# Emission order and per-tag buffer counts in a four-layer graph network kernel

## The chip, the cores and the metric

One Trainium2 chip, one core. The metric is the device time of one execution in microseconds (us). Lower is better. The kernel was already tuned. All runs told of here were in the same (fast) state, every kernel's output was correct, and each kernel has four timed runs (the kernel before, which was timed again with every call, seven in each later call).

A word on names. TensorE (PE in the profile) does the products and the transposes, VectorE (DVE) and ScalarE (ACT) do elementwise work, GpSimd (POOL) does a few small things. A *group* is four of the 128 graphs; there are 32 groups. An *accumulator* is one PSUM bank that a product writes and another engine reads. A *tag* is a name under which a pool keeps a ring of buffers: the n-th request for a tag with k buffers takes the place of request n - k, and must wait until that one is no longer used. An fp32 product shows as two matmul records in the trace, so a record count of 8 there means four products; a transpose shows as one record (the eight of a group's features as x8). The *granted clock* is the share of TensorE's full speed that the chip allowed it, as the trace records it.

## The reference, cut to what matters

Each of 128 graphs has 128 nodes with 256 features and an integer adjacency matrix. Four layers follow one another, each with a residual and a layernorm:

```python
x = _layernorm(x + _L0(x, adj, a0..a3))       # scores (x*a_k) x^T per edge type, softmax, times x
x = _layernorm(x + _L1(x, adj, W_msg, W_upd, bias))  # relu(x W_upd + mean of messages + bias)
x = _layernorm(x + _L2(x, adj, weight, w_ih, w_hh, ...))  # three GRU steps; each: aggregate A^T h, gates
x = _layernorm(x + _L3(x, adj, W, a))         # graph attention: softmax, times x W, elu
```

Within one graph everything depends on what went before. Different graphs are independent.

## The kernel before

All accumulators come from one PSUM tag with eight banks. All SBUF tiles of a group come from a pool with two buffers per tag unless a tile says otherwise.

```python
    work = ctx.enter_context(tc.tile_pool(name="work", bufs=2))
    psum = ctx.enter_context(tc.tile_pool(name="psum", bufs=8, space=bass.MemoryType.PSUM))

    def bank():
        return psum.tile([P, 512], F32, tag="ps", name="ps")
    ...
    def features_first(xn):                       # eight transposes, two banks
        xT = work.tile([P, KC, T], F32, tag="xT", name="xT")
        for c in range(KC):
            ps = bank()
            for b in range(G):
                nc.tensor.transpose(ps[:, b * N : (b + 1) * N], xn[:, b, c * P : (c + 1) * P], ident)
            ...
```

A group is a generator. It yields wherever TensorE would have to wait for another engine, and a small driver alternates between two groups that stand at different points:

```python
    def group(g):
        ...
        xT = features_first(xg)
        xs = work.tile([P, G, KC, 4, N], F32, tag="xs", name="xs", bufs=1)
        yield
        ...                                # scaled features, four edge types
        yield
        ...                                # scores, softmax, layernorm; layer 1; layernorm
        for i in range(NL):                # three recurrent steps
            ...                            # aggregation: 8 products of 128x128
            for c in range(KC):
                p_hn = gate(2 * KC + c, True, False)
                yield
                p_r = gate(c, True, True)
                ...
                yield
                p_in = gate(2 * KC + c, False, True)
                ...
        ...                                # layer 3

    STAGGER = 16
    running, g, step = [], 0, 0
    while running or g < NG:
        if g < NG and step >= g * STAGGER and len(running) < 2:
            running.append(group(g))
            g += 1
        for r in list(running):
            try:
                next(r)
            except StopIteration:
                running.remove(r)
        step += 1
```

## Time and profile before

| | before |
|---|---|
| time, median of 4 runs | 3757.63 us (3757.21 to 3757.7) |
| TensorE busy / idle in the span of 3756.9 us | 3353.8 / 403.1 us |
| granted TensorE clock, mean | 0.949 |
| one group, in the pairing (prediction's working) | about 116 us |

What TensorE waited for, from the view of waits of the kernel before. The columns are: what waited, what it waited for, us in all, how many times, and the longest.

```profile
PE ps L189 <- DVE xb L177: 163.7, 32, 8.6
PE ps L211 <- ACT prob L203: 77.3, 48, 4.0
PE ps L189 <- DVE xa L177: 67.8, 42, 4.5
PE ps L385 <- DVE hT L373: 29.3, 48, 2.1
```

There are 96 layernorms followed by transposes, 64 softmaxes and 96 ends of a recurrent step in the whole run. So the second column from the right shows how often the other group failed to cover: of the 96 step ends (L385) only 48 show a wait, of 0.6 us on average.

### The profile page before, as it was taken

What the parts mean: (1) busy time and instruction counts of PE and PEld (TensorE: products, weight loads), DVE (VectorE), ACT (ScalarE), POOL (GpSimd) and SP (SyncE); (2) the same over time, 40 slices, a digit from 0 to 9 for tenths busy, and PEclk for the clock granted to TensorE, in tenths of its full rate; (3) what the DMA queues carried; (4) which work ended last, traced back from release to release, by engine and by line L of the source; (5) the groups of instructions that cost most, each with busy time, mean ns of one, the idle gap of its engine ahead of it and who ended that gap; (6) DMA issues with size and microseconds to landing.
All of it is one profiled execution on the core that took longest, in us unless ns stands there. A gap on an engine that the chain in (4) does not pass through costs nothing.

```text
span 3756.9 us, 30963 instructions
## 1 busy us (share of the span) xinstructions
PE 3353.8 (89%) x10708; PEld 1804.6 (48%) x10708; DVE 2012.7 (54%) x5232; ACT 972.9 (26%) x2004; POOL 504.9 (13%) x487
## 2 busy tenths in 40 slices
PE   6998989889898898989989799898998989989896
PEld 4444444545454444545445444444444544445453
DVE  3456464564645546465464645546455464564644
ACT  2222222222222222232222222223222222222222
POOL 0111111111111111111111111111111111111111
PEclk8999999999999999999999899999999999999998
DMA  2000000000000000000000000000000000000000
GB/s 69 9 8 21 0 20 9 12 17 1 20 9 12 18 6 15 8 15 14 6 20 3 18 11 6 20 3 20 9 12 17 1 20 9 12 12 0 12 1 12
DMA packets 56957, 47.48 MB, mean 13 GB/s; under 512 B 4320, under 2 KB 56672, under 8 KB 56800
## 3 DMA queue, kind: packets, MB, share of 16 engines
q1 hardware_dynamic: 56800, 45.50, 3.9%
q8 instruction: 85, 1.39, 0.1%
q14 instruction: 72, 0.59, 0.0%
HBM read 28.72 MB, written 16.78 MB: 12 GB/s over the span
## 4 chain that ended last, share of the span: by engine, by line
PE 77%; DVE 14%; ACT 3%; issue 2%; POOL 2%; POOLq 0%; DVEq 0%; ACTq 0%
PE ps L342 48%; PE ps L290 6%; PE ps L250 6%; PE ps L328 5%; PE ps L189 4%; PE ps L406 3%; DVE st L170 2%; PE ps L385 2%; POOL rstd L174 2%; DVE hT L373 1%; DVE res L307 1%; PE ps L211 1%; DVE neg L441 1%; PE ps L437 1%; ACT t_z L368 1%
## 5 line engine op out<-in xcount | busy, mean ns | idle before, releaser
L342 PE MATMUL ps<-agT,c_gi 128*128 128x512 f32 x2304 | 1072.8, 595 | 0.0
L342 PE MATMUL ps<-hT,w_hhT 128*128 128x512 f32 x1536 | 753.2, 608 | 0.0
L342 PEld LDWEIGHTS ps<-agT,c_gi 128*128 128x128 f32 x2304 | 439.6, 191 | 552.4 <-issue 537.1
L372 DVE SCALAR_TENSOR_TENSOR t_d<-t_z,t_d 128x512 f32<-128x512 f32 x192 | 132.9, 692 | 501.7 <-ACT t_z L368 465.2
L342 PEld LDWEIGHTS ps<-hT,w_hhT 128*128 128x128 f32 x1536 | 280.7, 197 | 218.4 <-issue 214.8
L342 PE MATMUL ps<-xT,w_hhT 128*128 128x512 f32 x768 | 359.0, 593 | 0.0
L354 DVE TENSOR_SCALAR t_r<-t_r 128x512 f32<-128x512 f32 x192 | 81.6, 425 | 500.6 <-ACT t_r L353 500.6
L371 POOL TENSOR_TENSOR t_d<-hT,t_n 128x512 f32<-128x512 f32 x128 | 162.1, 1266 | 1031.8 <-ACT t_n L362 1031.8
L353 ACT ACTIVATE t_r<-ps,brz 128x512 f32<-128x512 f32 x192 | 131.6, 685 | 648.4 <-PE ps L342 648.4
L362 ACT ACTIVATE t_n<-t_r,bih 128x512 f32<-128x512 f32 x192 | 138.4, 721 | 455.5 <-DVE t_r L360 455.4
L290 PE MATMUL ps<-w_um,xT 128*128 128x512 f32 x512 | 231.2, 595 | 0.5 <-ACT xT L191 0.5
L250 PE MATMUL ps<-xs,xT 128*128 128x512 f32 x512 | 230.1, 592 | 1.7 <-ACT xs L245 1.7
L368 ACT ACTIVATE t_z<-ps,brz 128x512 f32<-128x512 f32 x192 | 131.3, 684 | 379.2 <-PE ps L342 379.2
L342 PEld LDWEIGHTS ps<-xT,w_hhT 128*128 128x128 f32 x768 | 142.3, 192 | 153.1 <-issue 145.8
L174 POOL TENSOR_TENSOR rstd<-rstd,neg_half 128x4 f32<-128x4 f32 x128 | 130.6, 1020 | 608.2 <-DVE rstd L173 603.2
L189 PE MATMUL ps<-ident,xb 128*128 128x128 f32 x256 | 53.4, 357 | 163.7 <-DVE xb L177 163.7
L258 DVE COPY_PREDICATED alpha<-mk,ps 128x128 f32<-128x128 uint8 x512 | 153.2, 300 | 81.4 <-PE ps L250 68.1
L191 ACT COPY xT<-ps 128x512 f32<-128x512 f32 x128 | 74.6, 583 | 420.6 <-PE ps L189 420.5
L360 DVE SCALAR_TENSOR_TENSOR t_r<-t_r,ps 128x512 f32<-128x512 f32 x192 | 131.5, 685 | 82.9 <-PE ps L342 79.2
L203 ACT ACTIVATE prob<-alpha,nmax 128x128 f32<-128x128 f32 x256 | 99.7, 391 | 264.6 <-DVE nmax L199 264.6
L371 POOL TENSOR_TENSOR t_d<-xT,t_n 128x512 f32<-128x512 f32 x64 | 81.0, 1266 | 620.3 <-ACT t_n L362 620.3
L406 PE MATMUL ps<-w3x,xT 128*128 128x257 f32 x512 | 153.7, 448 | 7.4 <-ACT xT L191 7.4
(95 smaller groups left out, 4045.0 us busy)
## 6 DMA issues: line engine op xcount, KB each, us to landing
x_in<-in_x_dram SPq DMA_DIRECT2D x32, 512.0 KB, 3.8
out_dram<-xb SPq DMA_DIRECT2D x32, 512.0 KB, 2.9
adj_in<-in_adj_dram SPq DMA_DIRECT2D x32, 256.0 KB, 2.8
nat<-in_L_gnn_w_hh_dram SPq DMA_DIRECT2D x1, 768.0 KB, 5.1
nat<-in_L_gnn_w_ih_dram SPq DMA_DIRECT2D x1, 768.0 KB, 6.8
wnat<-in_L_gnn_weight_dram SPq DMA_DIRECT2D x1, 768.0 KB, 7.7
w_um<-in_L_gnn_W_upd_dram SPq DMA_DIRECT2D x1, 256.0 KB, 3.4
w_um<-in_L_gnn_W_msg_dram SPq DMA_DIRECT2D x1, 256.0 KB, 3.6
```

The source lines that it names most:

```text
L174: nc.gpsimd.tensor_tensor(rstd, rstd, neg_half, OP.pow)
L189: nc.tensor.transpose(ps[:, b * N : (b + 1) * N], xn[:, b, c * P : (c + 1) * P], ident)
L250: nc.tensor.matmul(ps, xT[:, c, b * N : (b + 1) * N], xs[:, b, c].rearrange("p k n -> p (k n)"), start=(c == 0), stop=(c == KC - 1),)
L258: nc.vector.copy_predicated(alpha0[:, b, :], mk[:, k, b, :], ps[:, k * N : (k + 1) * N])
L290: nc.tensor.matmul(ps, xT[:, c, b * N : (b + 1) * N], w_um[:, c, :], start=(c == 0), stop=(c == KC - 1))
L328: nc.tensor.matmul(ps[:, b * N : (b + 1) * N], hn[:, b, c * P : (c + 1) * P], a_ne[:, b, :], start=True, stop=True,)
L342: nc.tensor.matmul(ps, w[:, q * P : (q + 1) * P], v, start=(n == 0), stop=(n == len(terms) - 1))
L362: nc.scalar.activation(t_n, t_r, AF.Tanh, bias=bih[:, 2 * KC + c : 2 * KC + c + 1], scale=1.0)
L368: nc.scalar.activation(t_z, p_z, AF.Tanh, bias=brz[:, KC + c : KC + c + 1], scale=0.5)
L371: nc.gpsimd.tensor_sub(t_d, hT[:, c, :], t_n)
L372: nc.vector.scalar_tensor_tensor(t_d, t_z, 1.0, t_d, op0=OP.add, op1=OP.mult)
L406: nc.tensor.matmul(ps[:, : D + 1], xT[:, c, b * N : (b + 1) * N], w3x[:, c, :], start=(c == 0), stop=(c == KC - 1),)
```

## The change

Its intent, in the words that came with it: groups emitted whole, oldest first, with buffers counted by tag so that three groups are in flight instead of two in lockstep. It has three parts: the yields and the driver go; every SBUF tag gets a buffer count of its own; and the scaled features of layer 0 are made in two halves that share one buffer. The core of the diff:

```diff
-    work = ctx.enter_context(tc.tile_pool(name="work", bufs=2))
+    pool = ctx.enter_context(tc.tile_pool(name="work", bufs=2))
...
+    BUFS = dict(
+        x_in=3, adj_in=2, a_f=2, mk=2, a_ne=3, m_gt=4, alpha=2, prob=2, probT=2,
+        xs=1, xT=3, hT=3, agT=3, hn=3, hu=1, x1=2, x2=3, x3=2, y=1, res=2,
+        t_r=3, t_n=3, t_z=2, t_d=2, mv=4, st=6, rstd=4, nmax=4, rsum=4, rinv=4, fac=6,
+    )
... (layer 0)
         xT = features_first(xg)
-        xs = work.tile([P, G, KC, 4, N], F32, tag="xs", name="xs", bufs=1)
-        yield
-        for c in range(KC):
+        for h in range(G // 2):
+            xs = work.tile([P, 2, KC, 4, N], F32, tag="xs", name="xs")
+            ...                        # scale two graphs, then their four score products
... (everywhere)
-        yield
...
-    STAGGER = 16
-    running, g, step = [], 0, 0
-    while running or g < NG:
-        ...
+    for g in range(NG):
+        group(g)
```

The weights' staging tiles also move from a pool of their own into the work pool. The PSUM tag is not touched.

## The prediction

> **What bounds the kernel now.** I read the page's first part and the chain that ended last, then the groups of instructions with the idle time before them, then TensorE's timeline at both ends of the run, then the granted clock by stretch.

> ```profile
> PE 3353.8 (89%) x10708; PEld 1804.6 (48%) x10708; DVE 2012.7 (54%) x5232; ACT 972.9 (26%) x2004; POOL 504.9 (13%) x487
> ...
> PE 77%; DVE 14%; ACT 3%; issue 2%; POOL 2%; POOLq 0%; DVEq 0%; ACTq 0%
> ```

> TensorE is busy for 89% of the span and carries 77% of the chain; the next engine is at 54%. So TensorE's own work is the floor, and about 3757 - 3354 = 403 us of its idle time is what a better interleaving could win. Some 23 us of the work is preparation, so a group of four graphs costs (3354 - 23) / 32 = 104 us of TensorE, and takes (3757 - 37) / 32 = 116 us in the present pairing. Nothing on the page shows what a group costs when no other group fills its waits. But two stretches do: the first group runs alone until the second enters at 91 us, and the last runs alone from 3693 us on. TensorE's timeline of the first (columns: start, length, instruction, and the idle time before it with what ended it):

> ```profile
> 37.14 1.04 PE L189 MATMUL ps<-ident,x_in 128*128 128x128 f32 x8
> 39.84 7.11 PE L250 MATMUL ps<-xs,xT 128*128 128x512 f32 x16 [1.67 <-ACT xs L245]
> 50.32 1.48 PE L211 MATMUL ps<-ident,prob 128*128 128x128 f32 x4 [3.37 <-ACT prob L203]
> 52.48 3.78 PE L271 MATMUL ps<-x_in,probT 128*128 128x256 f32 x8 [0.68 <-ACT probT L213]
> 60.81 1.94 PE L189 MATMUL ps<-ident,xa 128*128 128x128 f32 x8 [4.55 <-DVE xa L177]
> 63.20 8.25 PE L290 MATMUL ps<-w_um,xT 128*128 128x512 f32 x16 [0.46 <-ACT xT L191]
> 71.29 1.90 PE L300 MATMUL ps<-hu,a_f 128*128 128x257 f32 x8
> 80.50 2.10 PE L189 MATMUL ps<-ident,xb 128*128 128x128 f32 x8 [7.31 <-DVE xb L177]
> 82.39 3.62 PE L328 MATMUL ps<-a_ne,xb 128*128 128x128 f32 x16
> 85.80 3.68 PE L342 MATMUL ps<-xT,w_hhT 128*128 128x512 f32 x8
> ```

> Layers 0 and 1 of a lone group make TensorE wait for a softmax (3.37), a layernorm (4.55) and a mean with its layernorm (7.31). The last group, alone in its third recurrent step and layer 3:

> ```profile
> 3692.12 0.88 PE L385 MATMUL ps<-ident,hT 128*128 128x128 f32 x6 [0.68 <-DVE hT L373]
> 3693.53 2.05 PE L328 MATMUL ps<-a_ne,hn 128*128 128x128 f32 x16 [0.53 <-ACT hn L392]
> 3695.41 3.60 PE L342 MATMUL ps<-hT,w_hhT 128*128 128x512 f32 x8
> ...
> 3718.54 0.87 PE L385 MATMUL ps<-ident,hT 128*128 128x128 f32 x6 [2.14 <-DVE hT L373]
> 3723.93 1.97 PE L189 MATMUL ps<-ident,xa 128*128 128x128 f32 x8 [4.51 <-DVE xa L177]
> 3726.36 4.53 PE L406 MATMUL ps<-w3x,xT 128*128 128x257 f32 x16 [0.46 <-ACT xT L191]
> ...
> 3736.63 1.63 PE L211 MATMUL ps<-ident,prob 128*128 128x128 f32 x4 [4.03 <-ACT prob L203]
> 3738.94 3.78 PE L437 MATMUL ps<-wh,probT 128*128 128x256 f32 x8 [0.68 <-ACT probT L213]
> ```

> And the granted clock by stretch (third figure from the end; first row the lone first group, second the paired middle, third the lone last group):

> ```profile
> 37.00:86.00 49.00, 30.80 (x95) 18.70 (x94) 24.81 (x84) 9.06 (x23) 3.38 (x5) 0.76 0.07 17
> 1000.00:1200.00 200.00, 186.31 (x594) 98.79 (x595) 104.28 (x262) 51.07 (x100) 26.97 (x25) 0.97 0.03 10
> 3718.00:3745.00 27.00, 14.50 (x46) 9.71 (x46) 10.93 (x29) 6.35 (x19) 1.15 (x2) 0.69 0.00 1
> ```

> A lone group pays twice: it waits, and the clock falls from 0.97 to 0.76 or 0.69. The same eight transposes take 1.04 us at 37 us, and 1.94 to 2.10 after the long waits.

> [...] TensorE's records of before stand in the order of the built list wherever I compared them, and a waiting transpose (2.98 us at 3683.85) holds up gate products of the other group behind it. So if the list holds one group after another, no product of the next can fill a wait. [...] in half-microsecond stretches the clock is 1.00 or 0.50 but for the slices of a change; it drops at 51.7, returns at 65.0, drops at 75.3, returns at 85.5: about 13.4, 10.3 and 10.2 us apart, near whole multiples of 3.4.

> **The change part by part.** It removes every point where one group hands over to the other, calls the groups one after another, gives each tag its own number of SBUF buffers, and computes the scaled features of layer 0 in two halves through one buffer. The sum of products does not change: 6398 TensorE instructions in both built lists. The order does. The intent is that the scheduler overlaps three groups because their SBUF buffers allow it. But all accumulators are still one PSUM tag of 8 banks. In the built lists of both kernels the 2167 accumulators are first written in exactly the order in which the program asks for them, none out of order. Before, the program asked alternately for two groups. Now it asks for all of a group's banks before the next group's first, and the list of TensorE follows: the last product of group g (L431) comes before the first transpose of group g+1, 31 times of 31. So three groups are in flight only for loads and masks; on TensorE it is one. From group 5 to group 28 the lists of TensorE, VectorE, ScalarE and GpSimd repeat without a difference, so one period times 31 gives the time.

> A period, from the end of one group's last product to the next one's:
> (a) Layer 0 up to its last score product. Alone, at full clock, 39.84 + 7.11 - 37.14 = 9.8 us. Now the lists put the tail of the previous group (ELU, layernorm, output) among it, and VectorE's list puts the second half's scaling (128x256, estimated at 0.3 us from 0.48 for 128x512) behind that layernorm. The lone tail at the end of before starts writing its normalised output 3751.64 - 3742.72 = 8.9 us after the last product. Add about 1.9 because the ELU alternates with the next group's copies and scalings, 0.6 for predicated copies between, 1.4 for the four writes, 1.3 for four more predicated copies, 0.9 for scaling: the second half starts at about 15.0, after a wait of some 7 us, so at half clock. Four products of 0.86 us at full speed then take about 6.0. Estimate 21.0.
> (b) To the first gate product, as in the lone first group: 85.80 - 46.95 = 38.9.
> (c) Three recurrent steps of 24 gate products at 0.858: 3716.18 - 3695.41 = 20.8 each, 62.3.
> (d) Two inner step boundaries: 3718.54 - 3716.18 = 2.4 of wait, then 3695.41 - 3692.12 = 3.3 of transposes, copy and aggregation; 5.7 each, 11.3. [...]
> (e) Last step's end to the last product of layer 3: 3742.72 - 3716.18 = 26.5.
> Sum 161.5 us, against 116 now.

> The first group starts some 5 us later, as the second weight load must now wait for its one staging buffer: about 42. It has layer 0 alone with the halving's own wait (9.8 + 1.4) and b to e (140.5), so it ends at 194. Then 31 x 161.5 = 5006, and the lone tail of 3756.9 - 3742.7 = 14.2. Sum 5214; I say 5200. TensorE's busy share should be about 73%, its clock about 0.84.

> **The rivals.** One: the groups do overlap, as the change intends, and the 403 us of idle time mostly go: 3757 - 350 = about 3400. For it, VectorE's 54% leaves room; against it, the built order, with not one of 31 handovers mixed. Two: the order is serial, but the tail of a group hides fully behind the next one's layer 0 and the clock recovers quickly: (a) becomes about 11 and (d) has no surcharge, 150 a group, about 4850. Against it, the second half's scaling stands behind the previous layernorm in VectorE's list. Three: the waits of 2.4 us at step boundaries drop the clock nearly each time[...], about 5350. For it, the drop at 51.7 came in a window with only about 2.1 us idle; against it, the clock stood at 1.00 through the wait at 3716.4.

> **Range and chances.** All terms but (a) and the surcharge in (d) are read from the same instructions in the same order, at the clock that lone running gives. I leave 5 us a group upward (5214 + 150) and 7 downward (5214 - 217): 5000 to 5380. Faster would need the built order not to be the order run; 0.01. Within 2%: 0.01. Slower: 0.98.

> **What would show it.** In the profile after: TensorE's timeline repeats every 160 us or so with no product of another group within a group; waits of about 3.4, 4.6, 7.3, 2.1, 4.5 and 4.0 us before the softmax and layernorm transposes, once per group each; a wait of about 7 us amid the score products of layer 0; clock near 0.84; VectorE's busy time about unchanged at 2000. The prediction is wrong at its root if score products of one group stand among gate products of another, wrong in (a) if the wait amid the scores is far from 7 us, and wrong in (d) if the waits at step boundaries differ from 2.1 or the aggregation after them takes far over 2.05.

One term is cut: a surcharge of 1.5 us in (d), for waits at step boundaries that lower the clock; it was the author's guess. The sum includes it: 21.0 + 38.9 + 62.3 + 12.8 (11.3 and 1.5) + 26.5 = 161.5 us. What the trace of before shows of order and clock:

- Order: a transpose waited 2.98 us until 3683.85, and the other group's gate products behind it started at 3684.12.
- Clock: the clock record holds 50 stretches at 1.00 and 50 at 0.50, nothing else, and its changes lie on one grid with a step of 3.4133 us (to within 0.001 us). A window, in the prediction, is one such step. The window before the fall that the prediction puts at 51.7 (51.84 in the record) held 2.10 us of idle time.

The allowances in (a) are estimates. The mean durations in the trace of before to hold them against are 0.30 us for a predicated copy (L258), 0.41 for a write of a normalised output (L177) and 0.48 for a scaling of 128x512 (L243).

## The result, and the profile after

| | before | after |
|---|---|---|
| time, median of 4 runs each | 3757.63 us | 5178.01 us (5177.85 to 5180.56) |
| span of the profiled run | 3756.9 us | 5176.3 us |
| TensorE busy | 3353.8 us | 3837.8 us |
| TensorE idle (span less busy) | 403.1 us | 1338.5 us |
| granted clock, mean | 0.949 | 0.842 |

The ratio is 1.378 (95% interval 1.3761 to 1.38). Here and below a ratio is the mean time of one kernel's runs over the mean of the kernel before's runs of the same rounds, so it isn't quite the ratio of the medians. Later the kernel before had medians of 3756.64, 3758.0 and 3758.76 us. All outputs are right.

The page of the kernel after: the line of busy times, and the line of the chain that ended last.

```profile
PE 3837.8 (74%) x10708; PEld 2092.7 (40%) x10708; DVE 2024.9 (39%) x5359; ACT 1007.8 (19%) x2133; POOL 506.2 (10%) x487
...
PE 68%; DVE 19%; ACT 7%; POOL 4%; issue 2%; POOLq 0%; DVEq 0%; ACTq 0%
```

The number of TensorE records is the same, 10708, and VectorE's busy time has moved by 12 us. No work was added or taken away, yet TensorE is 484 us longer busy (3837.8 - 3353.8) and idle for 935 us more (1338.5 - 403.1). Together these are the 1419 us that the span grew. The second is waiting. The first is mostly the same products run at a lower clock, as experiment 5 will show (347 to 435 us of it).

The view of waits of the kernel after, to be laid beside that of before:

```profile
PE ps L205 <- DVE x L193: 509.1, 96, 7.3
PE ps L227 <- ACT prob L219: 237.0, 64, 4.4
PE ps L386 <- DVE hT L375: 204.1, 96, 2.4
PE ps L266 <- DVE xs L259: 198.8, 33, 6.3
PE ps L266 <- ACT xs L261: 55.5, 31, 1.8
```

The counts are now complete: every one of 96 layernorms, 64 softmaxes and 96 step ends makes TensorE wait. And there is a new row, the score products (L266) waiting for the scaled features: 6.3 us, once in every group.

One whole period in TensorE's timeline (start, length, instruction, and in brackets the idle time before it and what ended it). Most gate products and some other rows are left out.

```profile
1054.81 3.86 PE L347 MATMUL ps<-xT,w_hhT 128*128 128x512 f32 x8
...
1078.14 0.88 PE L386 MATMUL ps<-ident,hT 128*128 128x128 f32 x6 [2.08 <-DVE hT L375]
1079.36 3.60 PE L333 MATMUL ps<-a_ne,hn 128*128 128x128 f32 x16 [0.35 <-ACT hn L393]
1082.80 3.60 PE L347 MATMUL ps<-hT,w_hhT 128*128 128x512 f32 x8
...
1105.92 1.00 PE L386 MATMUL ps<-ident,hT 128*128 128x128 f32 x6 [2.14 <-DVE hT L375]
1107.14 3.38 PE L333 MATMUL ps<-a_ne,hn 128*128 128x128 f32 x16 [0.22 <-ACT hn L393]
1110.36 3.60 PE L347 MATMUL ps<-hT,w_hhT 128*128 128x512 f32 x8
...
1138.98 1.97 PE L205 MATMUL ps<-ident,x 128*128 128x128 f32 x8 [4.25 <-DVE x L193]
...
1152.20 1.63 PE L227 MATMUL ps<-ident,prob 128*128 128x128 f32 x4 [4.03 <-ACT prob L219]
1154.50 3.57 PE L431 MATMUL ps<-wh,probT 128*128 128x256 f32 x8 [0.68 <-ACT probT L229]
1157.91 1.04 PE L205 MATMUL ps<-ident,x_in 128*128 128x128 f32 x8
1160.74 4.07 PE L266 MATMUL ps<-xs,xT 128*128 128x512 f32 x8 [1.79 <-ACT xs L261]
1171.14 5.49 PE L266 MATMUL ps<-xs,xT 128*128 128x512 f32 x8 [6.33 <-DVE xs L259]
1179.99 1.48 PE L227 MATMUL ps<-ident,prob 128*128 128x128 f32 x4 [3.37 <-ACT prob L219]
...
1189.98 1.97 PE L205 MATMUL ps<-ident,x 128*128 128x128 f32 x8 [4.43 <-DVE x L193]
...
1209.93 2.10 PE L205 MATMUL ps<-ident,x 128*128 128x128 f32 x8 [7.25 <-DVE x L193]
...
1215.23 3.86 PE L347 MATMUL ps<-xT,w_hhT 128*128 128x512 f32 x8
```

Two things are to be seen. First, the row at 1157.91: the next group's first transposes come straight after the last product (L431) of the group before, and no product of one group stands among another's (the 332 TensorE matmul records from one group's first transposes to the next one's come in the same order 32 times of 32). Three groups are not in flight on TensorE; one is. Second, the aggregation (L333) takes 3.60 and 3.38 us after waits of 2.08 and 2.14 us. The same work took 2.05 us in the last group of before, at full clock.

In stretches of half a microsecond around these two aggregations, the third figure from the end is the granted clock:

```profile
1079.00:1079.50 0.50, 0.15 (x2) 0.14 (x1) 0.45 (x1) 0.31 (x1) 0.00 (x0) 0.72 0.00 0
1079.50:1080.00 0.50, 0.50 (x3) 0.50 (x4) 0.24 (x1) 0.00 (x0) 0.00 (x0) 0.50 0.00 0
...
1082.50:1083.00 0.50, 0.50 (x5) 0.49 (x4) 0.00 (x1) 0.00 (x0) 0.00 (x0) 0.86 0.00 0
...
1106.50:1107.00 0.50, 0.43 (x3) 0.06 (x1) 0.04 (x1) 0.49 (x1) 0.00 (x0) 0.53 0.00 0
...
1109.50:1110.00 0.50, 0.50 (x4) 0.50 (x4) 0.00 (x0) 0.32 (x1) 0.00 (x0) 0.56 0.00 0
```

A mean of 0.72 over 0.5 us is 0.22 us at full clock and 0.28 at half, so the clock fell at about 1079.22; worked out in the same way from the other rows it came back at 1082.64, fell again at 1106.53 and came back at 1109.94. Each stay at half clock lasts 3.41 or 3.42 us, and the falls are 27.31 us apart, eight times 3.41. So each of these two short waits is followed by one stay of 3.41 us at half clock, and the stays lie on one grid. The trace's clock record bears this out for the whole run: 252 stretches at 1.00 and 252 at 0.50, no other share, and all their changes on one grid with a step of 3.4133 us (to within 0.001 us); the kernel before has the same step. I call one step of this grid a window. The aggregation falls into it.

### The profile page after: what moved, and what is told of

Read it like the earlier page. It is cut to its first block, busy times and chain, and to the rows that moved or that the text cites. A ratio compares the mean times of both kernels' runs of the same rounds, so it can differ in the third digit from the quotient of the medians.

```text
span 5176.3 us, 31348 instructions
## 1 busy us (share of the span) xinstructions
PE 3837.8 (74%) x10708; PEld 2092.7 (40%) x10708; DVE 2024.9 (39%) x5359; ACT 1007.8 (19%) x2133; POOL 506.2 (10%) x487
## 4 chain that ended last, share of the span: by engine, by line
PE 68%; DVE 19%; ACT 7%; POOL 4%; issue 2%; POOLq 0%; DVEq 0%; ACTq 0%
PE ps L347 38%; PE ps L333 6%; PE ps L301 5%; PE ps L205 4%; PE ps L266 3%; DVE st L186 3%; PE ps L404 3%; POOL rstd L190 3%; PE ps L431 2%; PE ps L285 2%; DVE alpha L274 2%; POOL res L440 1%; DVE t_d L374 1%; ACT prob L219 1%; DVE hT L375 1%
## 5 line engine op out<-in xcount | busy, mean ns | idle before, releaser
L347 PE MATMUL ps<-hT,w_hhT 128*128 128x512 f32 x1536 | 701.1, 592 | 0.0
L205 PE MATMUL ps<-ident,x 128*128 128x128 f32 x768 | 193.1, 431 | 509.1 <-DVE x L193 509.1
L266 PE MATMUL ps<-xs,xT 128*128 128x512 f32 x512 | 299.7, 728 | 258.0 <-DVE xs L259 198.8
L205 PEld LDWEIGHTS ps<-ident,x 128*128 128x128 f32 x768 | 145.4, 213 | 557.6 <-DVE x L193 299.4
L373 POOL TENSOR_TENSOR t_d<-hT,t_n 128x512 f32<-128x512 f32 x128 | 162.2, 1267 | 1603.5 <-ACT t_n L365 1603.5
L386 PE MATMUL ps<-ident,hT 128*128 128x128 f32 x768 | 137.0, 308 | 204.1 <-DVE hT L375 204.1
L266 PEld LDWEIGHTS ps<-xs,xT 128*128 128x128 f32 x512 | 111.1, 234 | 427.6 <-issue 331.9
L301 PE MATMUL ps<-w_um,xT 128*128 128x512 f32 x512 | 272.2, 693 | 14.8 <-ACT xT L207 14.8
L227 PE MATMUL ps<-ident,prob 128*128 128x128 f32 x256 | 94.4, 402 | 242.4 <-ACT prob L219 237.0
L333 PE MATMUL ps<-a_ne,hn 128*128 128x128 f32 x1024 | 219.8, 402 | 17.9 <-ACT hn L393 17.9
L333 PEld LDWEIGHTS ps<-a_ne,hn 128*128 128x128 f32 x1024 | 207.6, 311 | 37.3 <-ACT hn L393 37.3
```

What stands on the lines that cost most here:

```text
L266: nc.tensor.matmul(ps, xT[:, c, b * N : (b + 1) * N], xs[:, j, c].rearrange("p k n -> p (k n)"), start=(c == 0), stop=(c == KC - 1),)
L301: nc.tensor.matmul(ps, xT[:, c, b * N : (b + 1) * N], w_um[:, c, :], start=(c == 0), stop=(c == KC - 1))
L333: nc.tensor.matmul(ps[:, b * N : (b + 1) * N], hn[:, b, c * P : (c + 1) * P], a_ne[:, b, :], start=True, stop=True,)
L347: nc.tensor.matmul(ps, w[:, q * P : (q + 1) * P], v, start=(n == 0), stop=(n == len(terms) - 1))
L373: nc.gpsimd.tensor_sub(t_d, hT[:, c, :], t_n)
```

## The experiments

The theory: TensorE runs its list in order (the waiting transpose at 3683.85 in the kernel before, and the 31 handovers of 31 in the kernel after, agree); with one PSUM tag, the order of the list is the order in which the program asks for banks; whole emission therefore makes TensorE do the groups one after another, each with all its waits, and the waits lower the clock as well (0.842 against 0.949). The rivals: the buffer counts or the halved scaling cost the time; the clock plays no part; it is some other resource than the banks that keeps the groups apart. Built instruction lists back the premise: in the kernels before and after, the 2167 accumulators are first written exactly in the order of the requests, none out of order.

### 1. Whole emission alone: old buffers, no halving

```diff
 # from the kernel before
-    STAGGER = 16
-    running, g, step = [], 0, 0
-    while running or g < NG:
-        ...
+    for g in range(NG):
+        for _ in group(g):
+            pass
```

> The kernel before with one change: each group's program is emitted to its end before the next one's begins; old buffers (two of each), layer 0's scaling in one piece. Theory (the order in which accumulators of the one PSUM tag are asked for sets TensorE's order, whatever the SBUF buffers are): serial, 5085 us, between 5000 and 5180; it lacks the wait amid layer 0's scores but has a longer one at the softmax behind. Rival (the new buffer counts or the halved scaling cost the time): within 3% of 3757.

Measured: 5064.37 us (5063.34 to 5064.59), ratio 1.3481 (1.3459 to 1.3504), clock 0.828. The order alone brings 1307 or 1308 of the 1420 us (5178.01 - 3757.63). On top of it the buffers and the halving add the other 114. The view of waits of this kernel shows where:

```profile
PE ps L250 <- ACT xs L245: 110.4, 32, 3.5
```

The score products wait 3.5 us once a group, where the kernel after waits 1.8 and 6.3 us, 254 us in all: there the second half of the scaling (L259) stands in VectorE's list behind the previous group's output (`y`, L193), as VectorE's timeline of the kernel after shows:

```profile
1168.09 1.38 DVE L193 TENSOR_SCALAR y<-res,mv,rstd 128x256 f32<-128x256 f32 x4 [1.00 <-POOL rstd L190]
1169.39 0.89 DVE L274 COPY_PREDICATED alpha<-mk,ps 128x128 f32<-128x128 uint8 x4
1170.18 0.35 DVE L259 TENSOR_SCALAR xs<-xT,acol 128x256 f32<-128x256 f32 x1
```

Of this difference of 144 us a part is given back, since TensorE is busy for 3881.6 us here and for 44 us less in the kernel after.

### 2. The new buffers and the halving alone: old order

```diff
 # from the kernel after: the yields and the old driver put back
+        yield
 ...
-    for g in range(NG):
-        group(g)
+    STAGGER = 16
+    while running or g < NG:          # two running, as before
+        ...
```

> The changed kernel with the old emission put back: two groups handing over to each other at the same points; buffers by tag, halved scaling and the new weight staging stay. Theory: 3757 within 2% (3690 to 3830), as nothing but the emission order matters. Rival (buffers and halving cost the time): above 4500.

Measured: 3758.03 us (3754.74 to 3762.24), ratio 1.0005 (0.999 to 1.002), clock 0.949. TensorE's busy time is that of before to within a microsecond, 3353.0 against 3353.8 us.

With two groups in alternation, the counts by tag are worth nothing, good or bad. Experiments 1 and 2 together leave the order as the cause.

### 3. Two PSUM tags by parity of the group

Is it the one ring of banks that fixes the order? Here even and odd groups ask for banks under different tags, four each. Everything is still emitted whole.

```diff
 # from the kernel after
+    lane = [0]
     def bank():
-        return psum.tile([P, 512], F32, tag="ps", name="ps")
+        return psum.tile([P, 512], F32, tag=f"ps{lane[0]}", name="ps", bufs=4)
...
     for g in range(NG):
+        lane[0] = g % 2
         group(g)
```

> The changed kernel with two PSUM tags of four banks, one for even and one for odd groups; SBUF tags still shared. Built list: 93 of 2167 accumulators first written out of emission order, about three a group, all at the handover (scores of layer 0 of the next group ahead of the softmax of layer 3). Theory (both kinds of tag hold the order; here only PSUM is loosened): waits at the handover partly filled, 4900 us, between 4780 and 5050. Rival (the PSUM tag alone is to blame): below 4000.

Measured: 4858.75 us, ratio 1.2935 (1.2915 to 1.2954), clock 0.843. In the built list there are now 93 places where an accumulator is first written after one that was asked for later. The timeline at a handover shows what they are:

```profile
1083.97 1.88 PE L413 MATMUL ps<-xT,w2b 128*128 128x512 f32 x4
1085.69 3.60 PE L268 MATMUL ps<-xs,xT 128*128 128x512 f32 x8
1090.32 1.49 PE L229 MATMUL ps<-ident,prob 128*128 128x128 f32 x4 [1.03 <-ACT prob L221]
...
1093.58 2.84 PE L433 MATMUL ps<-wh,probT 128*128 128x256 f32 x8
...
1106.13 1.63 PE L229 MATMUL ps<-ident,prob 128*128 128x128 f32 x4 [6.27 <-ACT prob L221]
```

The next group's scores (L268) fill the wait for the old group's last softmax (L229): 1.03 us of it is left, against 4.03. But this is given back at the younger group's own softmax, which now waits 6.27 us instead of 3.37, so that the softmax waits stay at 234.6 us in all, against 237.0. What is gained lies elsewhere: the waits amid the scores, 254 us in all in the kernel after, sink to 2.6, and TensorE is busy for 49 us less (3788.5). The younger group gets no farther than the scores of layer 0, since the SBUF tags are still shared by all groups, and the layernorm waits stay at 511.7 us, the step ends at 204.4.

### 4. SBUF tags by parity as well

```diff
 # from experiment 3
     BUFS = dict(
-        x_in=3, adj_in=2, ... xT=3, hT=3, agT=3, ...
+        x_in=1, adj_in=1, ... xT=1, hT=2, agT=1, ...     # mostly one buffer per lane
...
-            return pool.tile(shape, dtype, tag=tag, name=name, bufs=BUFS[tag])
+            return pool.tile(shape, dtype, tag=f"{tag}{lane[0]}", name=name, bufs=BUFS[tag])
```

> The changed kernel with PSUM and SBUF tags both by parity of the group, one buffer of most tags in each set. Groups are still emitted whole. Built list: score, update and aggregation products of a younger group stand among those of the older. Theory: real overlap of two groups, oldest first; TensorE's work of 3354 us plus 100 to 300 of waits: 3550, between 3430 and 3700. Rival (emission of whole groups is bad in itself, alternation is needed): 3757 or more.

Measured: 3996.42 us (3993.68 to 3997.22), ratio 1.0638 (1.0622 to 1.0654), clock 0.917. This missed what I expected, and fell where the rival had put it (3757 or more). The overlap is real: there are 218 such places in the built list, and 1182 of the 1420 us come back with nothing but tags by parity and smaller buffer counts. (The same SBUF lanes over one PSUM tag, which I built but did not run, leave 0 out of order. Both kinds of tag are needed.) But it is slower than the kernel before. Its timeline shows why it falls short:

```profile
1046.68 2.05 PE L270 MATMUL ps<-xs,xT 128*128 128x512 f32 x2 [11.43 <-DVE xs L263]
...
1052.89 3.60 PE L351 MATMUL ps<-xT,w_hhT 128*128 128x512 f32 x8
...
1073.71 2.74 PE L270 MATMUL ps<-xs,xT 128*128 128x512 f32 x6
```

The older group's recurrent steps, which are dense and need no help, run from 1052.89 on with 48 gate records to a step and nothing of the younger group between them; the younger one gets only a few score products where a step ends (1073.71). Then both groups stand in their waiting layers at once, and TensorE waits 11.43 us. The view of waits puts 320.7 us on that one place. "Oldest first" spends the overlap where it isn't needed; that this, and not the single buffers, is the cause is tested in experiment 9.

### 5. Waits filled with unread products

If the lower clock has a share of its own, then keeping TensorE busy in the waits, with products that nobody reads, must make the kernel faster although it adds work.

```diff
 # from the kernel after
+    def keep_warm(n):
+        ps = bank()
+        for _ in range(n):
+            nc.tensor.matmul(ps, w_um[:, 0, :P], w_um[:, 0, :], start=True, stop=True)
 ...   # keep_warm(3) ahead of softmax transposes, 4, 7 and 4 after x1, x2 and x3,
 ...   # 2 and 6 ahead of the halves of the scores, 2 ahead of each step's transposes
```

> The changed kernel with products that nobody reads put in TensorE's list ahead of its waits (2 to 7 of 0.86 us, each lot somewhat shorter than the wait), so that the clock has no reason to fall. Group order and waits stay. Theory: the 1419 us lost are 935 us of waits and 484 us of half clock (busy time 3838 against 3354); with the clock at 1.00 nearly throughout the time is 3354 + 1338 = 4690, between 4620 and 4800. Rival (the clock is only a companion, the waits in the chain set the time): 5178 within 1%.

Measured: 4863.87 us, ratio 1.2946 (1.2924 to 1.2967), clock 0.971. It is 314 us faster than the kernel after, with 1120 more products (two records each). I had expected more. The page, and the row of the unread products in the groups of instructions:

```profile
PE 4429.1 (91%) x12948; PEld 2230.3 (46%) x12948; DVE 2023.5 (42%) x5359; ACT 1005.8 (21%) x2133; POOL 505.7 (10%) x487
```

```profile
L73 PE MATMUL ps<-w_um 128*128 128x512 f32 x2240 | 1026.6, 594 | 0.0
```

Without the unread products, TensorE is busy for 4429.1 - 1026.6 = 3402.5 us, which is 435 less than the 3837.8 of the kernel after and only 49 more than the 3353.8 of before. This is the upper reading: the ends of products are modelled, and for 89 us the unread ones overlap their neighbours. Counted alone, the records of the other products cover 3491.3 us, which is 347 less than in the kernel after. So of the 484 us by which the products had grown longer, 347 to 435 go away when the clock is held up (0.971 against 0.842). With the upper reading, the span gains less because the filling isn't exact: the idle time falls from 1338.5 to 431.9 us, that is by 907, and the filling takes 1027, 120 too much. 435 - 120 = 315 us is the difference of the profiled spans (5176.3 - 4861.0). The expectation was in effect the whole 484 (5178 - 484 = 4694); the overrun of 120 and the 49 that stayed are what it lacked (with the lower reading, an overrun of 31 and 137 that stayed).

### 6. A second buffer for the scaled features

```diff
 # from the kernel after
-        xs=1, xT=3, hT=3, agT=3, ...
+        xs=2, xT=3, hT=2, agT=2, ...
```

> The changed kernel with two buffers for the scaled features of layer 0 (those for hT and agT cut to two). Built list: the second half's scaling now stands ahead of the previous group's layernorm, but the predicated copies of the scores still stand behind it. Theory: the wait of 6.3 us amid the scores goes, and most of it comes back at the softmax, because VectorE reaches the last copies only about 16.5 us after the previous group's last product: 3.5 us a group saved, 5070, between 5000 and 5130. Rival (the one buffer is the cause and its wait is gained whole with its clock, 8 us a group or more): below 4930.

Measured: 4965.72 us, ratio 1.3217 (1.3197 to 1.3237). The wait of 6.3 us amid the scores is gone, and part of it reappears as a longer wait for the softmax behind it:

```profile
1110.43 1.04 PE L205 MATMUL ps<-ident,x_in 128*128 128x128 f32 x8
1113.26 7.50 PE L266 MATMUL ps<-xs,xT 128*128 128x512 f32 x16 [1.79 <-ACT xs L261]
1127.43 1.63 PE L227 MATMUL ps<-ident,prob 128*128 128x128 f32 x4 [6.67 <-ACT prob L219]
```

From the first transposes to the softmax's it is 1127.43 - 1110.43 = 17.0 us here and 1179.99 - 1157.91 = 22.1 in the kernel after: 5.1 saved, where I had expected 3.5. The period fell by more still, 6.83 us, from 160.42 to 153.59; the trace shows the aggregation after the first step's end at 2.05 us instead of 3.60 in 31 of 32 groups, so part of the rest is clock. The time missed both what I expected (5000 to 5130) and the rival (below 4930). That this is twice 3.41 led to experiments 11 and 12.

### 7. Two groups in alternation, half a pass apart

```diff
 # from experiment 2
-    STAGGER = 16
+    STAGGER = 26
```

> Alternating emission of two groups as in the run that put the old order back, but each group starts 26 handovers after the one before it (half of a group's 51), where it was 16 and then 35 by turns. Theory: before's 403 us of idle time come from every second neighbour pair being in its waiting layers together; evenly offset, layers 0, 1 and 3 of one always lie beside the recurrent steps of the other: 3500, between 3420 and 3600. Rival (the offset does not matter): 3757 within 2%.

Measured: 3696.54 us, ratio 0.984 (0.9825 to 0.9854), clock 0.965. A gain of 61 us, clear of its interval, and a quarter of the expected one: idle time is still 344 us (3697.0 - 3353.1). The groups hand over at a count of yields, not of microseconds, so an offset of half the yields isn't half the time; that may be why, but no run shows it, and it stays open.

### 8. Three groups in alternation, new buffers

```diff
 # from experiment 2
-    STAGGER = 16
+    STAGGER = 17
...
-        if g < NG and step >= g * STAGGER and len(running) < 2:
+        if g < NG and step >= g * STAGGER and len(running) < 3:
```

> Alternating emission of three groups, 17 handovers apart, with the new buffer counts: what the change meant to have, three groups in flight. Theory: enough buffers for three; TensorE's idle time falls below that of two evenly offset groups: 3440, between 3390 and 3560. Rival (the counts are too small for three, waits for buffers take the place): 3650 or more.

Measured: 3556.43 us (3555.01 to 3556.98), ratio 0.9465 (0.9451 to 0.9479), clock 0.972: 5.4% faster than before, and the fastest kernel. It lies at the slow end of what I expected (3390 to 3560). Its page:

```profile
PE 3292.1 (93%) x10708; PEld 1786.6 (50%) x10708; DVE 2045.5 (58%) x5359; ACT 995.8 (28%) x2133; POOL 533.1 (15%) x487
```

A few rows of its timeline show gate products (L362) of two groups, one in its first step (its state is xT) and one in a later step (hT), with a third group's first transposes (x_in) ahead of them, and no wait:

```profile
1042.37 1.04 PE L205 MATMUL ps<-ident,x_in 128*128 128x128 f32 x8
1043.24 1.88 PE L362 MATMUL ps<-hT,w_hhT 128*128 128x512 f32 x4
1044.96 1.88 PE L362 MATMUL ps<-agT,c_gi 128*128 128x512 f32 x4
1046.68 1.88 PE L362 MATMUL ps<-xT,w_hhT 128*128 128x512 f32 x4
```

So what the change wanted, three groups in flight, is worth having. It has to be asked for in the order of emission.

### 9. The lanes of experiment 4 with alternating emission

```diff
 # from experiment 4: the yields put back, and
-    for g in range(NG):
-        lane[0] = g % 2
-        group(g)
+    STAGGER = 26
+    ...                               # the driver with two running; before each step
+            lane[0] = r[0]            # of a group, its parity
```

> PSUM and SBUF tags by parity of the group with one buffer of most, exactly as in the run with both kinds of lane, but the emission alternates between two groups 26 handovers apart instead of whole groups. Theory (in the run with lanes the groups were emitted whole, so every older product outranked the younger group's, which crept through layer 0 during the older's recurrent steps and then met it in its waiting layers): with alternation the younger gets its turns, 3690 or a little better, between 3600 and 3750. Rival (single buffers in each lane cost the time): 3950 to 4050 again.

Measured: 3604.88 us, ratio 0.9595 (0.9579 to 0.9611), clock 0.970. With the same tags and the same single buffers as experiment 4, alternating brings 392 us (3996.42 - 3604.88). So it was whole emission, oldest first, that held experiment 4 back, and not its small number of buffers. Tags by parity help under alternation too: experiment 7 alternates with the same offset but shared tags, has more buffers, and is 92 us slower (3696.54).

### 10. Three groups in alternation, old buffers

```diff
 # from the kernel before
-    STAGGER = 16
+    STAGGER = 17
...
-        if g < NG and step >= g * STAGGER and len(running) < 2:
+        if g < NG and step >= g * STAGGER and len(running) < 3:
```

> The kernel before with three groups in flight, 17 handovers apart, in place of two; its two buffers of each tag and its undivided scaling stay. Theory (three groups alternating need the counts of the change): tags with two buffers make the third group's instructions wait in TensorE's list, 3650 to 4000. Rival (only the emission matters, the counts do not): 3556 within 1%.

Measured: 3631.75 us, ratio 0.9666 (0.9652 to 0.9681), clock 0.967. It fell between what I expected and what the rival said. A third group helps even with two buffers a tag, by 3.3%; the counts by tag and the halving then bring a further 75 us (3631.75 - 3556.43; the intervals of the two ratios are far apart), the only place where they paid. With experiments 1, 2 and 8 the picture is a small table (medians in us):

| emission | old buffers | counts by tag, halved scaling |
|---|---|---|
| two in alternation | 3757.6 (before) | 3758.0 (exp. 2) |
| whole, oldest first | 5064.4 (exp. 1) | 5178.0 (after) |
| three in alternation | 3631.8 (exp. 10) | 3556.4 (exp. 8) |

### 11 and 12. One and two more products in every group

The mean period of groups 8 to 24, from the start of one group's first transposes to the next one's, came out near whole multiples of 3.4133 us, the step of the clock record in the kernels before and after, in kernels that differ in much else. These are the kernels whose means came out so:

| kernel | mean period, us | over 3.4133 |
|---|---|---|
| after | 160.421 | 47.00 |
| experiment 1 | 157.002 | 46.00 |
| experiment 3 | 150.186 | 44.00 |
| experiment 4 | 122.88 | 36.00 |
| experiment 6 | 153.588 | 45.00 |
| experiment 7 | 112.638 | 33.00 |

The others did not, or not cleanly: the quotients are 33.75 (before), 33.66 (experiment 2), 31.69 (8), 32.34 (9) and 32.54 (10), and in experiment 5 the mean gives 44.01 but single periods range from 149 to 151 us. So a lock is something that a kernel can have, not something that every kernel has.

If the period is locked to the windows, a little more work in each group costs either nothing or a whole window. So I put one and then two unread products of 0.86 us ahead of the first gate products, where TensorE doesn't wait:

```diff
 # from the kernel after
+            if i == 0:
+                unread = bank()
+                for _ in range(1):          # 2 in the second of the two kernels
+                    nc.tensor.matmul(unread, w_um[:, 0, :P], w_um[:, 0, :], start=True, stop=True)
```

> The changed kernel with one unread product of 0.86 us a group in TensorE's list ahead of the first gate products, where nothing waits. The period of the changed kernel is 160.43 us from group to group, 47.0 of the 3.413 us in which the clock changes, and other runs show 46.0, 45.0, 44.0, 36.0 and 33.0. Theory (each group's length settles on a whole number of clock windows): the period stays at 160.43 (5178 within 8) or becomes 163.84 (5284 within 10). Rival (a chance, work adds up): 5178 + 32 x 0.86 = 5205 within 5.

> The same with two unread products, 1.72 us a group. Theory: a period of 160.43 or 163.84 us, so 5178 within 8 or 5284 within 10. Rival: 5178 + 32 x 1.72 = 5233 within 5.

Measured: 5183.09 us (5181.39 to 5183.75), ratio 1.3793 (1.3773 to 1.3814), and 5192.13 us (5188.57 to 5194.1), ratio 1.3817 (1.3796 to 1.3838). Thirty-two times 0.86 and 1.72 us would be 28 and 55 us; the kernels became 5 and 14 us slower. The mean periods are 160.427 and 160.421, unchanged. The second kernel missed the locked expectation by 6 us, but it is far from the rival's. By the fifth group, before the lock settles, it has fallen 6.1 us behind the kernel after; from there to the thirtieth each group starts 6.08 to 6.14 us later than there, although every one of them has more work; and the last two groups add 6.7 us. Where the time is absorbed, the second kernel's timeline shows:

```profile
1060.90 2.15 PE L355 MATMUL ps<-w_um 128*128 128x512 f32 x4
1062.88 3.60 PE L347 MATMUL ps<-xT,w_hhT 128*128 128x512 f32 x8
...
1085.94 0.88 PE L390 MATMUL ps<-ident,hT 128*128 128x128 f32 x6 [2.08 <-DVE hT L379]
1087.16 2.05 PE L333 MATMUL ps<-a_ne,hn 128*128 128x128 f32 x16 [0.35 <-ACT hn L397]
```

The wait before the aggregation is 2.08 us as before, but the aggregation now takes 2.05 us and not 3.60: it came at another place on the grid and kept the full clock (the granted clock is 1.00 from 1087 to 1089 us). The same holds in 29 of 32 groups. So most of the added 1.7 us was taken out of time at half clock (3.60 - 2.05 = 1.55). The aggregation after the second step still ran at half clock, at 3.29 us in most groups.

Why the place on the grid matters can be counted from the traces, by adding up TensorE's idle time in each window of the recorded clock. In the kernel after, the window that ended at 1079.22 held 2.29 us of idle time and the one that ended at 1106.53 held 2.14, and after both the clock fell. In experiment 12 the wait was split between two windows, by an estimate from its timeline. Its transposes at 1112.18 took 1.16 us instead of 0.88, so the clock fell about 0.6 us before their end at 1113.34, at about 1112.8 (the same working puts the fall at 1106.53 of the kernel after 0.15 too late). Eight windows earlier, at 1085.3 to 1085.5, another window ended, amid the wait from 1083.86 to 1085.94; at most some 1.6 of its 2.08 us lay in one window, and the clock stayed.

## Why the prediction was right, point by point

The prediction was 5200 us; 5178.01 was measured. Its root was the reading of the built list: one PSUM tag, requests in program order, so one group at a time. Experiments 1 and 2 show that the order is what costs, and 3 and 4 that under whole emission the tags decide it.

| term, us per group | predicted | measured | read from |
|---|---|---|---|
| (a) layer 0 up to its last score product | 21.0 | 18.7 | 1157.91 to 1176.63 |
| (b) to the first gate product | 38.9 | 38.6 | 1176.63 to 1215.23 |
| (c) three steps of gates | 62.3 | 62.6 | 21.0 + 20.8 + 20.8 |
| (d) two inner step boundaries, with surcharge | 12.8 | 13.8 | 7.0 + 6.8 |
| (e) last step's end to the last product | 26.5 | 26.8 | 1131.1 to 1157.9 |
| sum | 161.5 | 160.5 (period 160.42) | |

- The waits that were named in advance came as named: 3.4, 4.4, 7.3, 2.1, 4.25 and 4.0 us against 3.4, 4.6, 7.3, 2.1, 4.5 and 4.0. They could be read off beforehand because the run before holds a lone group at either end. The first group's last product ended at 195.5 us (predicted 194) and the lone tail is 5176.3 - 5161.9 = 14.4 us (14.2).
- Term (a) was 2.3 us too high. The mechanism was as described (the scaling behind the previous group's output), but the allowances for VectorE's list were generous: the output's writes start 10.2 us after the first transposes (1168.09 - 1157.91), where the prediction adds up to 11.4, the second half of the scores after 13.2 us (1171.14 - 1157.91), where it had about 15.0, and these take 5.5 us instead of 6.0. The wait itself is 6.33 us for 7.
- Term (d) was 1 us too low. Its surcharge supposed that a wait of 2.1 us lowers the clock now and then; in the kernel after it does so at both boundaries of 30 of the 32 groups (3.60 and 3.38 us for the aggregation against 2.05). The prediction had the sign of it in hand, the fall after about 2.1 us of idle time; in the counts under experiment 12, every full-clock window of the kernel after with at least 2.08 us was followed by a fall. The third rival was right there about how often, and wrong about how much: (d) came out 1.0 us a group above the prediction, where its 5350 us needs some 4.7 (150 / 32).
- The first rival (overlap) fell with the timeline, and the second (period of 150, about 4850 us) with the wait amid the scores. Its hidden tail is what experiment 3 makes by other means, at 150.2 us a group.
- TensorE's share was 74% for the predicted 73%, the clock 0.842 for 0.84, VectorE 2024.9 us for "about 2000".
- Two slips in the working changed nothing: the clock changes of before, read from slices of half a microsecond, were at 51.84, 65.50, 75.73 and 85.97 us in the clock record, 13.65, 10.24 and 10.24 apart, which is four, three and three windows of 3.4133 us, where the text is only near them; and 5214 + 150 is 5364, not the 5380 of the range.

Two cautions on the good agreement of the sum. The errors partly cancel, which is luck: (a) was 2.3 us too high and (d) 1.0 too low. And the period is locked to a grid of 3.41 us, so small errors in the terms can't show in it: experiment 11 added 0.86 us to a group and the period did not move (160.427 us for 160.421). The terms are confirmed one by one from the timeline, not by the total.

What stays open: why half a pass of offset (experiment 7) gives only 61 us, and how much of the last 49 to 137 us of TensorE's longer busy time (experiment 5) is clock; what the rest would be, no run shows.

## What to carry to other kernels

Buffers permit overlap, but TensorE here overlapped only what its list interleaved (with whole emission over one PSUM tag, 31 handovers of 31 unmixed): before counting buffers, look at whether the list mixes two pieces of work, and look at every ring that both draw from, the PSUM banks too. Reach for alternating emission with a third piece of work in flight before whole emission, which gives the idle slots to the oldest work whether it needs them or not. And where the trace shows the clock fall after waits, count a wait twice, once as idle time and once as slower work after it (here 935 us and 347 to 435 us), and don't read gains smaller than a step of the clock record (here 3.41 us) from a single change before you have seen whether the period is locked (here 0.86 us more a group cost 5 us in all instead of 28).
